# An attention-and-feed-forward kernel on one core: a first unit with an order of its own, weight splits at other places, and layer norms measured and turned at other times

## The chip, the cores and the metric

The kernel runs on one core of one Trainium2 chip. The metric is the device time of one execution in microseconds (us), as the median of several runs. The engines are named as in the profile: PE (TensorE, matmuls), DVE (VectorE), ACT (ScalarE), POOL (GpSimd) and SP (SyncE, which here only issues transfers).

## The reference

The input x has 4 batches of 512 tokens and 512 features. The kernel adds two blocks to it.

```python
x = x + attn(layernorm(x))
x = x + ffn(layernorm(x))

# attn, with H = 16 heads, DK = 64, DV = 128, M = 64 slots
q, k, v, s, g = h @ Wq, h @ Wk, h @ Wv, clip(h @ Ws, -32, 32), h @ Wg
z  = cumlogsumexp(s over tokens);  p = exp(s - z);  decay = exp(z_prev - z)
hk_t = hk * decay_t + k_t p_t      # state 64 x 64 per head
ok_t = q_t hk_t;  pv = softmax(ok) # over the 64 slots
hv_t = hv * decay_t + p_t v_t      # state 64 x 128 per head
o_t  = pv_t hv_t
o = o * rsqrt(mean(o*o) + 1e-5) * g_norm_weight * silu(g)
attn = o @ Wo

# ffn, 512 -> 1536 -> 512, weights rounded to float8_e4m3 first
ffn = (silu(h @ gate * gs) * (h @ up * us)) @ down * ds
```

All values are float32.

## The kernel before

**Units.** Attention is cut into 32 units. A unit is one group g of two heads (g from 0 to 7) for one batch b. The first half goes through all groups with batches 0 and 1 in turn: unit 0 is (g 0, b 0), unit 1 is (0, 1), unit 2 is (1, 0), and so on to unit 15, which is (7, 1). Units 16 to 31 do the same with batches 2 and 3. A unit with even g also computes the values v for two groups, so it is longer. After unit 31 comes the feed-forward block: 4 batches, each in 12 chunks of 128 hidden features.

**A unit.** The function `attention` writes a unit down in this order: projections s (`slots`), k (`keys`) and q (`queries`); transposes of e = exp(s) and k; for even g the four parts of v (`values`); the states and masked products of the first recurrence (`key_states`, `query_key`); the gate g of two heads (`gate_main`, `gate_mixed`, `gate_silu`); `slot_scores` (ok), the softmax, the second recurrence and `read_out` (ov). The output of the unit before is finished inside the next one: `scale_output`, `turn_output`, `high_output` and `split_output` make its oT, and `project_output` multiplies by Wo (ps_o in the profile; `add_output` adds ps_o_m and sends y to the `stream` in DRAM with an accumulating transfer of POOL).

**Precision.** A float32 product is made of three products in fp32r. A weight or an activation is split into a high part, a low part and a third one, called less. A projection is then eight matmuls of high and low parts (`main`, ps_g for instance) and four with the third (`mixed`, ps_g_m). A projection has its own PSUM tile from a pool of three (ps3, "proj"), so a third one after `main` waits until ACT has evicted the first. Unit 0 alone multiplies in plain float32 (`whole`), with the raw weights and with `xn_whole`, the normed tokens.

**Weight splits.** `load_matrix(nm, g, True)` splits a matrix in pieces of 512 columns: `high` on ACT (L245) and `rest`, two operations on DVE (L252 and L257), so w_s, w_k and w_q have one piece, w_g and w_o two, w_v four. The raw matrix comes by `fetch`, two buffers in turn. The split matrix is also stored to DRAM (split_*), and the second half loads it from there (L231).

**Layer norms.** `layernorm(b, which)` measures each of the four 128-token chunks (`measure`: three DVE operations and a power on POOL), normalises (xn), transposes on PE (ps_xn) and splits the result in `parts` (xs; DVE L349 and L351, ACT L354). x_0 is measured and turned before anything else. x_2 is measured in unit 14 and turned in unit 15. x_3 is loaded and measured at the start of unit 16. x_0 of the second norm is measured in unit 30.

**Order.** Nothing is scheduled by a tool: with `tc.manual_schedule` each engine carries out its instructions in the order in which they are written. Two lists fill that order. `work` holds pieces of weight splits, layer norm measures, xs parts and the rounding of feed-forward weights: `other(n)` carries out the next n pieces (or `pace[0]` of them), and `need(name)` goes on until no piece of that name is left. `steps` holds the transposes of a layer norm, one chunk in each `next_step()`. In the second half the feed-forward weights are rounded to float8 in such pieces on DVE (`quantize`) and stored to `rounded`.

Of the kernel before, what the change touches and what calls it, by code (L numbers as in the profile page):

```python
# [49 lines left out]
def kernel(  # L50
# [18 lines left out]
    nc = tc.nc  # L69
# [101 lines left out]

    def need(key):

        while any(name == key for name, _ in work):
            other(1)
# [31 lines left out]
    def fetch_first():  # L207

        for tag, names in (("og", "sk"), ("oT", "q"), ("w_o", "g")):
            w = one.tile([P, 2, RAW // 2], F32, tag=tag, name=f"raw_{names}")  # L210
# [8 lines left out]
            if names == "q":  # L219
                fetch()  # L220
                fetch()

    def load_matrix(nm, g, first):
# [23 lines left out]
        def rest(n):  # L247
# [10 lines left out]
            if (n + 1) * 512 % RAW == 0 or n + 1 == pieces:  # L258
                if g > 0 or nm in "vo":
                    fetch()  # L260
# [12 lines left out]
        work.append((nm, lambda: high(0)))  # L273
# [22 lines left out]
    def layernorm(b, which, n_bank=None):  # L296
# [33 lines left out]
        def transposes(n):  # L330
# [6 lines left out]
            if which == 1:  # L337
# [5 lines left out]
        def parts(n):  # L343
# [3 lines left out]
            if start:  # L347
                src = whole[0][:, :, cols]
            nc.vector.tensor_tensor(lo, src, hi, ALU.subtract)  # L349
# [6 lines left out]
        if start:  # L356
            for n in range(NT):
                measure(n)
                if n > 0:
                    normalise(n - 1)  # L360
                    transposes(n - 1)
            normalise(NT - 1)
# [6 lines left out]
        at = max([i + 1 for i, (name, _) in enumerate(work) if name in ("v", "g", "q")], default=0)  # L369
# [139 lines left out]
    def project(nm, b, name, to, between=None):  # L509
        if name == f"{nm}_0_0":  # L510
            p = Projection(nm, b, 0, name).whole()
            other({"s": 6, "k": 2, "q": 2}[nm])
# [85 lines left out]
    class Heads:  # L598
# [195 lines left out]
        def split_output(self, h):  # L794
# [4 lines left out]
            )  # L799
            nc.scalar.mul(lo, lo.bitcast(F32), 1.0 / DELTA)  # L800
# [30 lines left out]
    def attention(g, b, before, load):  # L831
# [5 lines left out]
        def output(n):  # L837
            if before:
                before.project_output(n)
                before.add_output(n)  # L840
# [6 lines left out]
        if before:  # L847
            need(f"xs_{b}")
            need("s")
# [4 lines left out]
        if before:  # L854
            before.scale_output()
            need("k")

        def running_sum():
            if before:
                before.scale_other()  # L860
# [7 lines left out]
        if before:  # L868
            need("q")
        X.queries(other if before and (even or steps) else None)  # L870
        load("q")
        X.turn_e()
        if even:
            X.turn_k()
            if before:
                need(f"xs_{b}")
                need("v")
                need("xs_0")
            X.values(0)
            if before:  # L880
                before.turn_output(0)
# [4 lines left out]
            next_step()  # L886
            if before:
                before.high_output(0)
                before.split_output(0)
                before.turn_output(1)  # L890
            X.query_key()
            X.values(2)
            if before:
# [305 lines left out]
```

## Time and profile before

| | before |
|---|---|
| median of 3 runs | 1541.26 us (1541.14 to 1542.71) |
| the profiled execution | 1541.84 us, of which the span of the core is 1540.0 |
| mean granted TensorE clock | 0.987 |
| idle time of PE | 68.5 us |
| DVE, ACT, POOL busy | 72%, 46%, 13% of the span |
| chain that ended last | PE 81%, DVE 13%, ACT 4%, issue 2% |
| DMA | 212.5 MB, mean 138 GB/s |

The span is the stretch from the first to the last instruction of the core; 1.84 us of the execution lie around it. The page counts the time that an engine worked. A busy PE need not be at full speed: PEclk is the clock granted to it, in tenths. A unit's place in time is read from the first ps_s of the unit in the timeline of PE.

### The profile page before, as it was taken

The page shows a single profiled execution, that of the slowest core. Times are in us where ns is not written, and L with a number is a line of the kernel's source. Part 1 is how long each engine was busy: PE and PEld are TensorE (multiplying, and loading weights), DVE is VectorE, ACT ScalarE, POOL GpSimd, SP SyncE. Part 2 cuts the span into 40 slices and gives each one's busy share as a digit, 9 for nine tenths or more (in the row PEclk, how much of TensorE's full clock was granted, in tenths as well). Part 3 has the DMA queues.
Part 4 walks back from the last instruction along what each step waited for, and adds up shares of the span by engine and source line. Part 5 has one row for each costly group of instructions (what it writes and reads, how often), then busy time and mean ns, then how long its engine had stood idle before and what let it go on. Part 6 is the DMA issues. An engine that isn't in the chain of part 4 may idle for free.

```text
span 1540.0 us, 23008 instructions
## 1 busy us (share of the span) xinstructions
PE 1471.5 (96%) x9053; PEld 1180.2 (77%) x9053; DVE 1109.0 (72%) x1968; ACT 708.3 (46%) x1214; POOL 193.0 (13%) x204
## 2 busy tenths in 40 slices
PE   7897999999999999699999999999999999999998
PEld 3576778778887887577778877887888778888886
DVE  5676767886788678757788888888888865444333
ACT  3544454655555455434554454444544543222222
POOL 2001101111121102101110111111111211000000
PEclk9998999999999999989999999999999999999999
DMA  6235645475557464505673668265836562101000
GB/s 233 103 116 164 180 157 153 118 214 189 160 130 230 123 243 106 178 1 151 192 200 68 178 187 222 63 244 137 234 99 234 125 195 28 38 18 55 1 28 28
DMA packets 80715, 212.52 MB, mean 138 GB/s; under 512 B 6152, under 2 KB 34848, under 8 KB 75424
## 3 DMA queue, kind: packets, MB, share of 16 engines
q1 hardware_dynamic: 61792, 176.96, 31.4%
q0 software_dynamic: 18528, 33.58, 15.1%
q8 instruction: 71, 1.16, 0.3%
q10 hardware_dynamic: 288, 0.52, 0.1%
q14 instruction: 36, 0.29, 0.1%
HBM read 107.23 MB, written 108.00 MB: 140 GB/s over the span
## 4 chain that ended last, share of the span: by engine, by line
PE 81%; DVE 13%; ACT 4%; issue 2%; DMA 0%; POOL 0%; DVEq 0%; POOLq 0%; ACTq 0%
PE ps_o L810 8%; PE ps_v L540 7%; PE ps_fg L970 5%; PE ps_fu L970 5%; PE ps_ov L737 4%; PE ps_o_m L810 4%; PE ps_g L480 4%; PE ps_v_m L540 3%; PE ps_q L480 3%; PE ps_g_m L503 3%; PE ps_s L480 3%; PE ps_k L480 3%; PE ps_fd L1014 2%; PE ps_a L567 2%; PE ps_fe L1014 2%; PE ps_b L567 2%
## 5 line engine op out<-in xcount | busy, mean ns | idle before, releaser
L826 POOL DMA_DIRECT2D stream<-y x128 | 110.9, 869 | 933.4 <-DVE y L825 901.3
L810 PE MATMUL ps_o<-w_o,oT 128*128 128x512 f32 x512 | 150.5, 413 | 6.0 <-DVE w_o L252 5.2
L820 ACT ACTIVATE y<-ps_o 128x512 f32<-128x512 f32 x128 | 76.7, 599 | 134.2 <-PE ps_o L810 132.4
L480 PE MATMUL ps_g<-xs,w_g 128*128 128x512 f32 x496 | 127.2, 398 | 5.9 <-ACT w_g L245 5.3
L540 PE MATMUL ps_v<-w_v,xs 128*128 128x512 f32 x480 | 126.2, 405 | 0.0
L991 DVE SCALAR_TENSOR_TENSOR h<-ps_fu,scol,act 128x512 f32<-128x512 f32 x48 | 36.0, 750 | 108.3 <-PE ps_fu L970 107.0
L480 PEld LDWEIGHTS ps_g<-xs,w_g 128*128 128x128 f32 x496 | 92.6, 190 | 27.4 <-ACT w_g L245 5.9
L810 PEld LDWEIGHTS ps_o<-w_o,oT 128*128 128x128 f32 x512 | 89.7, 189 | 26.2 <-DVE w_o L252 6.8
L540 PEld LDWEIGHTS ps_v<-w_v,xs 128*128 128x128 f32 x480 | 87.6, 190 | 19.6 <-issue 0.2
L800 ACT ACTIVATE oT<-oT 128x512 fp32r<-128x512 f32 x64 | 40.6, 634 | 130.9 <-DVE oT L797 130.9
L970 PE MATMUL ps_fg<-xs,wf 128*128 128x512 f32 x384 | 96.8, 394 | 2.0 <-DVE xs L349 2.0
L970 PE MATMUL ps_fu<-xs,wf 128*128 128x512 f32 x384 | 95.0, 389 | 0.0
L825 DVE TENSOR_TENSOR y<-y,ps_o_m 128x512 f32<-128x512 f32 x128 | 87.3, 682 | 8.4 <-ACT y L820 5.5
L970 PEld LDWEIGHTS ps_fg<-xs,wf 128*128 128x128 f32 x384 | 71.1, 188 | 16.7 <-DVE xs L349 2.3
L970 PEld LDWEIGHTS ps_fu<-xs,wf 128*128 128x128 f32 x384 | 72.1, 188 | 15.2
L810 PE MATMUL ps_o_m<-w_o,oT 128*128 128x512 f32 x256 | 81.0, 396 | 1.7 <-ACT y L820 1.7
L507 DVE TENSOR_TENSOR sg<-sg,ps_g_m 128x512 f32<-128x512 f32 x62 | 42.6, 687 | 45.2 <-PE ps_g_m L503 42.3
L549 DVE TENSOR_TENSOR v<-v,ps_v_m 128x512 f32<-128x512 f32 x60 | 41.2, 686 | 46.9 <-PE ps_v_m L540 42.6
L997 ACT CAST both<-h 128x512 fp32r<-128x512 f32 x48 | 30.0, 624 | 96.6 <-DVE h L991 96.6
L480 PE MATMUL ps_s<-xs,w_s 128*128 128x512 f32 x248 | 66.1, 408 | 8.5 <-ACT xs L354 8.5
L503 PE MATMUL ps_g_m<-xs,w_g 128*128 128x512 f32 x248 | 68.7, 399 | 4.5 <-ACT sg L485 4.5
L752 POOL TENSOR_TENSOR rs<-rs,mhalf 128x8 f32<-128x8 f32 x32 | 58.9, 1839 | 103.4 <-DVE rs L749 95.5
(165 smaller groups left out, 3216.9 us busy)
## 6 DMA issues: line engine op xcount, KB each, us to landing
stream<-y POOLq DMA_DIRECT2D x128, 256.0 KB, 5.8
split_v<-w_v SPq DMA_DIRECT2D x4, 3072.0 KB, 11.4
split_g<-w_g SPq DMA_DIRECT2D x8, 1536.0 KB, 7.1
split_o<-w_o SPq DMA_DIRECT2D x8, 1536.0 KB, 6.2
w_v<-split_v SPq DMA_DIRECT2D x4, 3072.0 KB, 15.4
w_g<-split_g SPq DMA_DIRECT2D x8, 1536.0 KB, 6.7
w_o<-split_o SPq DMA_DIRECT2D x8, 1536.0 KB, 10.1
rounded<-qw SPq DMA_DIRECT2D x36, 256.0 KB, 4.2
```

The costliest lines, as they stand in the source:

```text
L480: nc.tensor.matmul(self.p, products(self.nm, c, self.col0, i), xs[self.b][i][:, c, :], start=(i == 0 and c == 0), stop=(i == 1 and c == KC ...
L503: nc.tensor.matmul(self.m, products(self.nm, c, self.col0, 2), xs[self.b][2][:, c, :], start=(c == 0), stop=(c == KC - 1),)
L540: nc.tensor.matmul(dst, xs[b][i][:, c, n * P : (n + 1) * P], wt["v"][:, i, c * 2 * HV : (c + 1) * 2 * HV], start=(i == which[0] and c == 0 ...
L567: nc.tensor.matmul(pa[h][:, n, :], lT[rows, cols], rT[rows, cols], start=True, stop=True)
L737: nc.tensor.matmul(po[h][:, n, :], self.bb[h][:, n, :], both_v[self.b][:, n, self.v0 + h * DV : self.v0 + (h + 1) * DV], start=False, stop ...
L752: nc.gpsimd.tensor_tensor(rs, rs, mhalf.rearrange("p (h n) -> p h n", h=HG), ALU.pow)
L810: nc.tensor.matmul(dst, self.oT[:, i, h, n * P : (n + 1) * P], wt["o"][:, i, h * D : (h + 1) * D], start=(i == which[0] and h == 0), stop= ...
L820: nc.scalar.mul(y, p, 1.0 + DELTA)
L825: nc.vector.tensor_tensor(y, y, m, ALU.subtract)
L826: nc.gpsimd.dma_start(stream[self.b][n * P : (n + 1) * P, :], y, accum_op=ALU.add)
L970: nc.tensor.matmul(pp, w[:, c * P : (c + 1) * P], xs[b][k][:, c, :], start=(c == 0 and k == 0), stop=(c == KC - 1 and k == 1),)
L1014: nc.tensor.matmul(sums[n], parts[k][:, n * P : (n + 1) * P], fw[c][2], start=(c == 0 and k == 0), stop=(c == NFC - 1 and k == 1),)
```

## The change

- `first_unit` writes unit 0 down by itself. The first part of its values is computed between the second and the third transpose of x_0, the second before s; the gate of the first head comes before ok, that of the second after the softmax. The raw Wv is fetched ahead of Ws, Wk and Wq, and all four chunks of x_0 are loaded from SP. The high part of xs_0 is made from `xn_whole` in `parts`, no longer right after the transpose.
- The splits of the first weights are queued at the start of unit 0 (s, k, q, v, then the parts of xs_0, then g; o later), and carried out along units 0 and 1. `piece` carries out the high part and the first rest of a matrix together. Odd-g units begin with `piece()` in place of two `other(1)`, and `pace` is 2 only at unit 1 and at unit 16. So the later splits of the first half also stand at other places: that of g for unit 14 directly before its gate, that of o in unit 15 directly before ps_o.
- `split_output` gives its ACT scaling to `low_output`; in odd-g units it is written behind `gate_main(0)`.
- x_2 is measured from unit 13 on and turned from `gated()` of unit 14, which stands between the gate's projections and `gate_silu`. x_3 is loaded and queued at `gated()` of unit 15, and turned in unit 16. The second norm of x_0 is measured from unit 29 on and turned from `gated()` of unit 30.

```diff
                 work.pop(0)[1]()
+    def piece():
+        while work:
+            name, run = work.pop(0)
+            run()
+            if not name.endswith("_"):
+                break
     def need(key):
...
     def fetch_first():
+        fetch()
+        fetch()
         for tag, names in (("og", "sk"), ("oT", "q"), ("w_o", "g")):
+            if names == "g":
+                load_tokens(1, x)
             w = one.tile([P, 2, RAW // 2], F32, tag=tag, name=f"raw_{names}")
...
                 )
                 raw[nm, 0] = [to]
-            if names == "q":
-                fetch()
-                fetch()
...
             nc.vector.scalar_tensor_tensor(w[:, 2, cols], hi, DELTA, lo, ALU.mult, ALU.subtract)
             if (n + 1) * 512 % RAW == 0 or n + 1 == pieces:
-                if g > 0 or nm in "vo":
+                if g > 0 or nm == "o":
                     fetch()
...
             rest(n)
-        work.append((nm, lambda: high(0)))
+        work.append((nm + "_", lambda: high(0)))
         work.extend((nm, lambda n=n: step(n)) for n in range(pieces))
...
             if start:
                 src = whole[0][:, :, cols]
+                nc.scalar.mul(dst[0][:, :, cols], src, UNDER)
             nc.vector.tensor_tensor(lo, src, hi, ALU.subtract)
...
                     normalise(n - 1)
                     transposes(n - 1)
+                if n == 2:
+                    between()
             normalise(NT - 1)
...
         todo.insert(2, (key + "0", lambda: normalise(0)))
         todo.insert(4, (key + "1", lambda: normalise(1)))
-        at = max([i + 1 for i, (name, _) in enumerate(work) if name in ("v", "g", "q")], default=0)
+        at = max([i + 1 for i, (name, _) in enumerate(work) if name in ("v", "g", "q") or name[:3] == "xs_"], default=0)
         work[at:at] = todo
...
         if name == f"{nm}_0_0":
             p = Projection(nm, b, 0, name).whole()
-            other({"s": 6, "k": 2, "q": 2}[nm])
             nc.scalar.mul(to, p, QSCALE if nm == "q" else 1.0)
...
                 less, lo.bitcast(F32), -1.0 / DELTA, hi.bitcast(F32), ALU.mult, ALU.add
             )
+        def low_output(self, h):
+            lo = self.oT[:, 1, h, :]
             nc.scalar.mul(lo, lo.bitcast(F32), 1.0 / DELTA)
...
         nc.scalar.preload_act_table_set("natural_log_exp_and_others")
-    def attention(g, b, before, load):
+    def first_unit():
+        X = Heads(0, 0)
+        parts = layernorm(0, 1, between=lambda: X.values(0))
+        for nm in "skqv":
+            load_matrix(nm, 0, True)
+        transposing = layernorm(1, 1)
+        work.extend(parts)
+        load_matrix("g", 0, True)
+        for _ in range(5):
+            piece()
+        X.values(1)
+        X.slots()
+        other(2)
+        X.keys(X.running_sum)
+        other(4)
+        X.queries(None)
+        X.turn_e()
+        X.turn_k()
+        piece()
+        piece()
+        X.values(2)
+        X.key_states()
+        piece()
+        X.inverse()
+        X.values(3)
+        fetch()
+        fetch()
+        load_matrix("o", 0, True)
+        transposing()
+        next_step()
+        other(2)
+        X.query_key()
+        next_step()
+        other(2)
+        X.gate_main(0)
+        piece()
+        X.slot_scores()
+        X.value_states()
+        next_step()
+        X.softmax()
+        X.softmax_exp()
+        other(1)
+        next_step()
+        other(1)
+        X.gate_main(1)
+        X.slot_weights()
+        X.gate_silu(0)
+        X.gate_silu(1)
+        exp_and_log()
+        X.weight_slot()
+        X.softmax_sum()
+        need("xs_0")
+        X.read_out()
+        return X
+    def attention(g, b, before, load, gated):
         X = Heads(g, b)
         even = g % 2 == 0
         def output(n):
-            if before:
-                before.project_output(n)
-                before.add_output(n)
+            before.project_output(n)
+            before.add_output(n)
         def early_step():
             if not any(name.endswith("_m") for name, _ in work):
                 next_step()
-        if before:
-            need(f"xs_{b}")
-            need("s")
+        need(f"xs_{b}")
+        need("s")
         X.slots()
         load("s")
         if not even:
             early_step()
-        if before:
-            before.scale_output()
-            need("k")
+        before.scale_output()
+        need("k")
         def running_sum():
-            if before:
-                before.scale_other()
+            before.scale_other()
             X.running_sum()
...
             before.split_output(1)
             X.inverse()
-        if before:
-            need("g")
-            X.gate_main(0)
-            X.gate_mixed(0)
-            if even:
-                other()
-                next_step()
-            X.gate_main(1)
-            X.gate_mixed(1)
-            load("g")
-            if even:
-                load("v")
-            X.gate_silu(0)
-            X.gate_silu(1)
-            exp_and_log()
+        need("g")
+        X.gate_main(0)
+        if not even:
+            before.low_output(0)
+            before.low_output(1)
+        X.gate_mixed(0)
+        if even:
+            other()
+            next_step()
+        X.gate_main(1)
+        X.gate_mixed(1)
+        load("g")
+        if even:
+            load("v")
+        gated()
+        X.gate_silu(0)
+        X.gate_silu(1)
+        exp_and_log()
         X.slot_scores()
         X.value_states()
-        if not before:
-            next_step()
-            X.gate_main(0)
         X.softmax()
         other()
-        if before:
-            need("o")
-            before.project_output(0)
+        need("o")
+        before.project_output(0)
         X.softmax_exp()
-        if before:
-            before.add_output(0)
-            before.project_output(1)
-        else:
-            X.gate_main(1)
-            X.gate_silu(0)
-            X.gate_silu(1)
-            exp_and_log()
-            load("v")
-            load("g")
+        before.add_output(0)
+        before.project_output(1)
         X.slot_weights()
-        if before:
-            before.add_output(1)
+        before.add_output(1)
         X.softmax_sum()
-        if before:
-            next_step()
+        next_step()
         output(2)
...
         x1[0] = one.tile([P, NT, D], F32, tag="y", name="x1_0")
         for n in range(NT):
-            (nc.scalar if n % 2 else nc.sync).dma_start(x1[0][:, n, :], blocks[:, n, :])
+            nc.sync.dma_start(x1[0][:, n, :], blocks[:, n, :])
         exp_and_log()
         fetch_first()
-        parts_0 = layernorm(0, 1)
-        for nm in "skq":
-            load_matrix(nm, 0, True)
-        load_tokens(1, x)
         for b in range(2):
             nc.sync.dma_start(stream[b], x[b])
         load_scales()
         units = [(g, b) for b0 in range(0, B, 2) for g in range(NG) for b in (b0, b0 + 1)]
-        before = None
+        before = first_unit()
+        scale_columns()
         to_come = [3 * NFC]
-        for i, (g, b) in enumerate(units):
-            last = i + 1 == len(units)
+        for i, (g, b) in enumerate(units[1:], 1):
             def load(nm):
                 after = (i + 1 + 2 * (nm == "v")) // 2 * 2
-                if i == 0:
-                    if nm in "vgo":
-                        load_matrix(nm, 0, True)
-                    if nm == "v":
-                        work.extend(parts_0)
-                    return
                 if b == B - 1 and after == len(units):
                     for c, tag in enumerate(PLACES):
                         if tag == f"w_{nm}":
                             load_ffn(c)
                 elif nm == "o":
-                    if b % 2 == 0 and i > 0:
+                    if b % 2 == 0:
                         load_matrix("o", g, i < len(units) // 2)
                 elif b % 2 == 1 and after < len(units):
                     n = units[after][0]
                     load_matrix(nm, n // 2 if nm == "v" else n, after < len(units) // 2)
+            def gated():
+                pace[0] = 1 + (pace[0] > 1 and i > 1)
+                if g == NG - 1 and b % 2 == 0:
+                    transposing[0]()
+                elif (g, b) == (NG - 1, 1):
+                    need("xs_2")
+                    load_tokens(3, x)
+                    transposing[0] = layernorm(3, 1)
...
             if (g, b) == (NG - 2, 2):
                 load_tokens(0, stream)
+            if (g, b) in ((NG - 2, 1), (NG - 2, 3)):
+                transposing = [layernorm(*((2, 1) if b == 1 else (0, 2)))]
             if (g, b) == (0, 2):
-                load_tokens(3, x)
-            if i == 0 or (g, b) == (0, 2):
-                layernorm(b + 1, 1)()
-            elif (g, b) in ((NG - 1, 0), (NG - 1, 2)):
-                transposing = layernorm(*((2, 1) if b == 0 else (0, 2)))
-            elif g == NG - 1:
-                transposing()
-            if (g, b) == (0, 2):
+                transposing[0]()
                 assert not to_fetch
                 stage()
             if b > 1:
                 for _ in range(min(0 if units[i] == (0, 2) else 2 if g % 2 else 4 if b == 2 else 3, to_come[0])):
                     work += [("round", f) for f in quantize()]
                     to_come[0] -= 1
-            pace[0] = 2 if steps else 1
-            if before:
+            pace[0] = 2 if i == 1 or (g, b) == (0, 2) else 1
+            if g % 2:
+                piece()
+            else:
                 other(1)
                 other(1)
-            before = attention(g, b, before, load)
-            while steps:
-                next_step()
-            if i == 0:
-                scale_columns()
+            before = attention(g, b, before, load, gated)
         dsc = one.tile([P, D], F32, tag="qT", name="dsc")
```

## The prediction, on record before the result

> **What bounds the kernel now.** I read the page first: the busy row of TensorE (PE), then the forty slices.
>
> ```profile
> span 1540.0 us, 23008 instructions
> PE 1471.5 (96%) x9053; PEld 1180.2 (77%) x9053; DVE 1109.0 (72%) x1968; ACT 708.3 (46%) x1214; POOL 193.0 (13%) x204
> ...
> PE   7897999999999999699999999999999999999998
> ...
> PEclk9998999999999999989999999999999999999999
> ```
>
> PE is the bound: 96%, 68.5 us idle. The low digits lie at the start (slices 1 to 5) and in slice 17 (about 650 us), where the granted clock dips too. So the work that DVE and ACT do elsewhere is hidden, and only these two places can pay. Next the waits of PE, its own list, columns "waited for: total, times, longest":
>
> ```profile
> PE ps_s L480 <- ACT xs L354: 8.5, 1, 8.5
> PE ps_xn L333 <- DVE xn L326: 7.8, 3, 7.1
> PE ps_g L480 <- ACT w_g L245: 5.3, 2, 5.1
> PE ps_o L810 <- DVE w_o L252: 5.2, 5, 1.5
> PE ps_q L480 <- ACT w_q L245: 5.0, 2, 2.5
> PE ps_g_m L503 <- ACT sg L485: 4.5, 15, 0.4
> PE ps_k_m L503 <- ACT eT L485: 3.9, 1, 3.9
> PE ps_a L567 <- DVE xs L349: 3.2, 1, 3.2
> ```
>
> Seven of the eight are single stalls; one (ps_g_m) comes back in every odd-g unit. The timeline places them. On PE, the bracket is the idle time before the row:
>
> ```profile
> 68.44 2.07 PE L503 MATMUL ps_k_m<-xs,w_k 128*128 128x512 f32 x4 [3.91 <-ACT eT L485]
> 135.07 3.78 PE L480 MATMUL ps_g<-xs,w_g 128*128 128x512 f32 x8 [5.09 <-ACT w_g L245]
> ...
> 654.60 2.08 PE L480 MATMUL ps_s<-xs,w_s 128*128 128x512 f32 x4 [8.46 <-ACT xs L354]
> ...
> 677.83 3.78 PE L540 MATMUL ps_v<-w_v,xs 128*128 128x512 f32 x8
> ```
>
> A warm group of eight takes 1.98 to 2.1 us; the eight at 135.07 and 677.83 take 3.78. A long stall is paid twice: once idle, once at half clock. Last, the SyncE queue (SP) ahead of the 8.46 us stall:
>
> ```profile
> 628.29 0.32 SPq L231 DMA_DIRECT2D w_g<-split_g  x1
> 634.45 0.32 SPq L265 DMA_DIRECT2D split_o<-w_o  x1
> 634.82 0.43 SPq L291 DMA_DIRECT2D x<-_attn_hidden_states_dram  x1
> ```
>
> The 1 MB load of x_3 starts at 634.82 and lands 9.6 us later.
>
> To price stalls with their half clock, I take the distance between the first ps_s of consecutive units. Undisturbed, an even-g unit (with values) takes 41.8 us, an odd-g unit 31.7 (first batch of the pair) or 32.7 (second). Measured: unit 0 ends at 59.7; unit 1 53.7 (excess 11.9), unit 2 42.7 (11.0), unit 3 37.6 (4.9), unit 4 44.6 (2.8), unit 15 37.4 (4.7), unit 16 62.9 (21.1, of which 1.4 is x_3's four transposes). Together 56 us.
>
> **What the Trainium skill says.** "TensorE: Matmul & The Clock Gate", section "Part 1: The HAM clock gate": after an idle window of about 3.4 us the array goes to half clock, and needs about 3.4 us of sustained work to get the full one. The trace agrees: after the stalls the clock is down for 3.41 us (from 122.5), 6.83 (67.9, 132.7 and 675.4) and 10.24 (648.0). The same page, "Engine queue depths", has ACT and DVE strictly first in, first out; so does the trace, where ACT's eviction of eT (68.44 above) stands behind four w_v splits that start at 58.36. "Trainium Kernel Development and Optimization", section "Key Constraints": transfers issued from SP, ACT and POOL share 16 DMA engines, and a second issuer saves issue time only. So x_0's chunks all on SP cost two issues, 0.4 us each, hidden behind the first two chunks' measures.
>
> **The change part by part.** PE and DVE issue the same instructions in both kernels. ACT gives two DMA issues to SP. All is order.
>
> *Start.* In the old order the first projection, s, begins at 12.89, after all four transposes of x_0 (from 7.10 on) and 0.67 for ACT's copy. Now v_0_0 needs only two of them: they end at 9.67, so v_0_0 begins near 10.3. raw_v, now issued ahead of s, k and q at about 2.1 and 2.9 instead of 3.34 and 4.2, lands 6.8 later, at 8.9 to 9.7, in time. But the other eight transposes (2.17) are moved behind v_0_0 and not saved; what goes is the idle between groups, 0.4, and, as PE works densely from 10.3 on, perhaps one cold window of 3.41 us (the clock rose at 16.7), worth 1.7. I take −2 (+1 if raw_v lands with s's traffic at 11.5; −4 if the windows fall well).
>
> *Units 1 to 4.* W_V's eight DVE operations (0.65 each) and four ACT highs (0.62 each) leave the end of unit 0 for its early part, where PE runs 3.5 us whole-fp32 projections and DVE has room. W_G is split at the end of unit 0, W_O in unit 1, each ahead of its use. In exchange x_0's parts now end unit 0 (four DVE operations, 2.7 us), and w_g's two highs stand before eT on ACT. Unit 1: of the 11.9 excess, stay about 1.5 to 2.4 of the 3.9 stall with some half clock, and the rest of the crowded DVE (6 operations of about 0.65 between z and qT, as before). I take −6.5 (−3 to −9). Unit 2: the waits for w_q (2.5) and w_g (5.1), with 1.7 and 3.4 lost to half clock, have their cause removed, both splits done in unit 1. −10.5 of 11.0 (−6 to −11). Unit 3: w_o split before kT instead of between ok and y; −4.5 of 4.9. Unit 4: w_q's high ahead of eT, the 2.5 us wait goes: −2.5. If that cover fails, the wait for w_q's last low part, one 0.65 operation, is what is late next.
>
> *low_output.* In odd-g units the two ACT scalings of oT (0.63 each) go behind sg's eviction, which PE waits for 15 times at 0.3. Two of those units are counted above: 13 x 0.3 = −4.0. What is late next is oT itself, needed only at ps_o, 6 us later.
>
> *Units 8 and 12.* w_q's pair now stands before kT: +0.3 each, +0.5 in all.
>
> *Unit 14 (new wait).* W_G's four DVE operations leave unit 13's end, for the place between rzT and sg of unit 14. There DVE ends rzT at 593.33 in the old frame, while ps_g began at 588.08. The low parts come at 593.9 and 595.2, the last at 595.9. So the gate's main group ends near 596.0 instead of 590.0: 6.0, less 0.3 of the old sg wait, plus about 1.5 of half clock after 4 to 5 us idle: +7 (+3 to +9). Behind it wait sg, ok, and everything after.
>
> *Unit 15 (new wait).* x_3's load is moved before gate_silu. It is queued on SP behind w_g's load, which waits for PE's last ps_g_m (628.29). It is issued at about 628.7 instead of 634.8; w_g (1.5 MB, 6.3 us alone) shares the engines, so I take 9 us and a landing near 637.7 (6.3 and 9.6 bound it: 635.0 to 638.3). DVE ends ok at 633.06; the next in its queue are four measures of x_3 (1.0 each), two xn (0.5 each) and W_O's four operations (2.6). The measures wait for the load, so they end at 642.8, and W_O at 645.4. ps_o's second half waits for it: its mixed pair ends at 645.9, was 634.8. +11.1. The rest of the unit (10.2) is shorter by the 0.5 wait and two transposes (0.7), longer by about 3 of half clock after 12 us idle. +12.9; I take +13 (+7 to +16).
>
> *Unit 16.* Its xs_2 is ready. The stall of 8.46, that of 3.16 at 675.85, and both cold stretches go. ACT's y wait (1.7) and the transposes remain: 62.9 to about 45.4, −17.5 (−13 to −19).
>
> *Feed-forward start.* The old waits of 0.5 and 2.0 for xs_0 go, but eight quantising operations (about 5 us) come in front of h_0 on DVE. 0 (−2 to +2).
>
> **Sum**: −2.0 −6.5 −10.5 −4.5 −2.5 −4.0 +0.5 = −29.5 for the first half; +7 +13 −17.5 = +2.5 for the handover. −27.0. The profiled execution took 1541.84 (span 1540.0); it becomes 1514.8. That execution is 0.6 above the median, so **1514.2**.
>
> **Rivals.** *The handover pays.* x_3 lands at 635, PE's clock stays up, and unit 14's gate waits only 3: units 14 and 15 cost +3 and +7 instead of 20, and the rest holds. That is 10 less: 1504.2. For it: x chunks of 256 KB landed in 4.1 us. Against it: the measures and W_O alone are 7.6 us of DVE in front of ps_o.
>
> *The splits only change place.* The operation counts are the same; DVE in unit 1 is 77% busy (41.1 of 53.7 us). If the stalls of units 1 to 3 come back at kT and qT in half their size, 21.5 becomes 10.7: 1525.0. Against it: unit 2 was 70% busy, and it is not the load but one position in ACT's queue that made its waits.
>
> *Slower: x_3 comes very late.* One mechanism: DVE is in order, and the measures stand ahead of W_O and y in unit 15, so PE loses one us for each us that x_3 lands later than my 637.7. The gain of 27 is gone at a load of 36 us; 45 us give 1550.2. Against it: the longest median landing on the page is 15.4 (w_v, 3 MB), and x_3 took 9.6 in the same traffic.
>
> *That the change does not do what it says* is the second rival at its full size for the first half: nothing but the start and the sg waits, −2.0 −4.0 +0.5 +2.5 = −3.0, 1538.3.
>
> **How the numbers follow.** Forecast 0.62 (1505 to 1523), handover pays 0.16, splits change place 0.17 (with 0.03 for the full size), slower 0.04, about nothing 0.01. 0.2% is 3.1 us, about what a measurement of this kernel can tell from no change. Faster 0.94, same 0.02, slower 0.04. The range reaches into both neighbours: 1499 to 1529.
>
> **What would show it.** Right: first ps_v near 10.3 and unit 1's first ps_s near 57.7; unit 2 of about 32 us; no ps_g_m wait for sg; a new PE wait of 4 to 6 us for w_g in unit 14, and one of 7 to 13 us for w_o in unit 15, with DVE's first measure of x_3 waiting about 4.6 us for a DMA; unit 16 of about 45 us without ps_s or ps_a waits. Wrong: w_q or w_g waits left in unit 2, kT or qT late in unit 1, a short ps_o wait in unit 15 (then 1504), or one beyond 20 us.

## The result, and the profile after

The changed kernel takes 1537.36 us (median of 12, 1535.66 to 1540.92), the kernel before 1541.49 beside it (12 runs): ratio 0.9973, interval 0.9964 to 0.9982. It is 4.1 us faster, where 27 were forecast. The profiled execution took 1536.70, its span is 1534.7 (5.3 less than before).

The page of the changed kernel, busy row of PE, its forty slices and the clock:

```profile
span 1534.7 us, 23020 instructions
PE 1462.3 (95%) x9053; PEld 1177.2 (77%) x9053; DVE 1109.1 (72%) x1968; ACT 710.4 (46%) x1214; POOL 192.7 (13%) x204
...
PE   8899999999999978799999999999998899999998
...
PEclk9999999999999999899999999999999999999999
```

The digits at the start rose from 7897 to 8899. The dip at slice 17 is still there and wider (7, 8, 7 from slice 15 on), and a dip is new at slices 31 and 32. The sum of PE's idle time rose from 68.5 to 72.4 us (1534.7 − 1462.3), so the kernel is not faster because PE waits less: PE is busy for 9.2 us less with the same 9053 matmuls. The mean granted clock of 0.989, which was 0.987, makes about 3 of that (an estimate, 0.002 of 1540); e6 below shows another part, rows that overlap again. The waits of PE, columns "waited for: total, times, longest":

```profile
PE ps_o L825 <- DVE w_o L262: 10.1, 2, 9.6
...
PE ps_g L493 <- DVE w_g L262: 4.8, 2, 4.6
...
PE ps_q L493 <- DVE w_q L264: 3.1, 3, 1.6
...
```

The old list's stalls at ps_s (8.5) and ps_a (3.2) are gone, and so are the fifteen waits of ps_g_m for sg. Waits for w_q, w_g and w_o are still there in name, but at another place in time. The distance between the first ps_s of consecutive units, from the timeline of PE, says where (us; for unit 31 up to the first ps_fg, then to the end of the span):

| stretch | before | after | difference | forecast |
|---|---|---|---|---|
| start of unit 1 | 59.70 | 58.43 | −1.3 | −2 |
| unit 1 | 53.67 | 47.85 | −5.8 | −6.5 |
| unit 2 | 42.66 | 31.08 | −11.6 | −10.5 |
| unit 3 | 37.63 | 31.04 | −6.6 | −4.5 |
| unit 4 | 44.64 | 42.99 | −1.7 | −2.5 |
| units 8 and 12 | 83.59 | 88.03 | +4.4 | +0.5 |
| units 5, 6, 7, 9, 10, 11, 13 | 254.1 | 249.6 | −4.4 | in −4.0 |
| unit 14 | 31.67 | 42.33 | +10.7 | +7 |
| unit 15 | 37.35 | 53.96 | +16.6 | +13 |
| unit 16 | 62.93 | 47.82 | −15.1 | −17.5 |
| units 17 to 29 | 483.0 | 481.9 | −1.2 | in −4.0 |
| unit 30 | 31.69 | 38.33 | +6.6 | 0 |
| unit 31 | 34.17 | 37.16 | +3.0 | 0 |
| first ps_fg to the end | 283.2 | 284.2 | +1.0 | 0 |

Each column is one execution. Stretches without a new wait agree within 0.1 us from run to run. The others do not: unit 0, written the same in ten further profiles below, takes 57.2 to 59.6, and unit 8 43.7 to 46.9 in the runs that leave its order alone.

Up to unit 14 the changed kernel is 26.9 us ahead (575.94 against 549.04). The handover, units 14 to 16, costs 12.2 of it, and the tail from unit 30 on another 10.6. On PE's timeline of the changed kernel, the bracket again the idle time before the row:

```profile
557.29 2.12 PE L493 MATMUL ps_q<-xs,w_q 128*128 128x512 f32 x8 [2.51 <-ACT w_q L255]
569.92 1.07 PE L493 MATMUL ps_g<-xs,w_g 128*128 128x512 f32 x2 [4.56 <-DVE w_g L262]
...
601.27 1.08 PE L343 MATMUL ps_xn<-ident,xn 128*128 128x128 f32 x4 [3.68 <-DVE xn L336]
...
632.41 0.80 PE L825 MATMUL ps_o<-w_o,oT 128*128 128x512 f32 x1 [9.61 <-DVE w_o L262]
...
1184.74 3.57 PE L493 MATMUL ps_q<-xs,w_q 128*128 128x512 f32 x8 [4.00 <-DVE eT L520]
```

Two of these, the waits for w_g and w_o, are the ones that the forecast announced. The other three it did not have. DVE's timeline shows what makes the longest:

```profile
621.64 0.69 DVE L704 TENSOR_TENSOR ok<-ps_okn,mx 128x512 f32<-128x512 f32 x1
626.68 0.69 DVE L329 BATCH_NORM_STATS2 stats<-x 128x6 f32<-128x512 f32 x1 [4.35 <-DMA x<-_attn_hidden_states_dram]
...
631.66 0.69 DVE L262 TENSOR_TENSOR w_o<-raw_o,w_o 128x512 fp32r<-128x512 f32 x1
```

After ok DVE waits 4.35 us for x_3's load (issued at 617.94, landed in 8.7), measures for 5.0, and only then splits w_o, for which PE has waited since 622.8. The tail has the same pattern. First the SP queue, then DVE:

```profile
1161.85 0.32 SPq L241 DMA_DIRECT2D w_g<-split_g  x1
1162.21 2.04 SPq L473 DMA_DIRECT2D wf<-rounded  x4
1164.35 0.41 SPq L421 DMA_DIRECT2D qw<-in_L_ffn_gate_w_dram  x1
```

```profile
1183.32 0.43 DVE L437 TENSOR_SCALAR q<-qw 128x512 int32<-128x512 int32 x1 [6.52 <-DMA qw<-in_L_ffn_gate_w_dram]
...
1184.00 0.68 DVE L520 TENSOR_TENSOR eT<-eT,ps_s_m 128x512 f32<-128x512 f32 x1
```

A raw feed-forward weight of 256 KB is issued behind 4.5 MB on the same queue and lands after 18.9 us. The rounding piece that needs it stands in front of eT on DVE, and with eT the whole of unit 30. In the kernel before the same four loads were issued at 1178.1, and of the rounding only one last store came after them:

```profile
1178.09 2.26 SPq L460 DMA_DIRECT2D wf<-rounded  x4
1189.44 0.32 SPq L438 DMA_DIRECT2D rounded<-qw  x1
```

### The profile page after: what moved, and what is told of

It reads as the page before. It is cut to its first block, busy times and chain, and to the rows that moved or that the text cites. A ratio compares the mean times of both kernels' runs of the same rounds, so it can differ in the third digit from the quotient of the medians.

```text
span 1534.7 us, 23020 instructions
## 1 busy us (share of the span) xinstructions
PE 1462.3 (95%) x9053; PEld 1177.2 (77%) x9053; DVE 1109.1 (72%) x1968; ACT 710.4 (46%) x1214; POOL 192.7 (13%) x204
## 4 chain that ended last, share of the span: by engine, by line
PE 81%; DVE 9%; DMA 5%; ACT 3%; issue 1%; SPq 0%; DVEq 0%; ACTq 0%
PE ps_o L825 7%; PE ps_v L552 7%; PE ps_g L493 7%; PE ps_fg L1023 5%; PE ps_fu L1023 5%; PE ps_q L493 4%; PE ps_g_m L516 3%; PE ps_o_m L825 3%; PE ps_ov L749 3%; PE ps_v_m L552 3%; PE ps_s L493 3%; PE ps_k L493 2%; PE ps_fd L1067 2%; PE ps_fe L1067 2%; PE ps_a L579 2%; PE ps_b L579 2%
## 5 line engine op out<-in xcount | busy, mean ns | idle before, releaser
L825 PE MATMUL ps_o<-w_o,oT 128*128 128x512 f32 x512 | 149.7, 413 | 11.1 <-DVE w_o L262 10.1
L493 PEld LDWEIGHTS ps_g<-xs,w_g 128*128 128x128 f32 x496 | 92.1, 189 | 26.9 <-DVE w_g L262 6.0
L1023 PEld LDWEIGHTS ps_fu<-xs,wf 128*128 128x128 f32 x384 | 72.1, 188 | 15.2
L498 ACT ACTIVATE sg<-ps_g 128x512 f32<-128x512 f32 x62 | 37.1, 599 | 98.6 <-PE ps_g L493 98.6
L493 PE MATMUL ps_q<-xs,w_q 128*128 128x512 f32 x248 | 66.7, 412 | 9.9 <-DVE eT L520 4.3
L1041 ACT ACTIVATE act<-ps_fg,scol 128x512 f32<-128x512 f32 x48 | 33.0, 688 | 80.3 <-PE ps_fg L1023 80.3
## 6 DMA issues: line engine op xcount, KB each, us to landing
w_v<-split_v SPq DMA_DIRECT2D x4, 3072.0 KB, 15.2
```

What stands on the lines that cost most here:

```text
L493: nc.tensor.matmul(self.p, products(self.nm, c, self.col0, i), xs[self.b][i][:, c, :], start=(i == 0 and c == 0), stop=(i == 1 and c == KC ...
L825: nc.tensor.matmul(dst, self.oT[:, i, h, n * P : (n + 1) * P], wt["o"][:, i, h * D : (h + 1) * D], start=(i == which[0] and h == 0), stop= ...
L1023: nc.tensor.matmul(pp, w[:, c * P : (c + 1) * P], xs[b][k][:, c, :], start=(c == 0 and k == 0), stop=(c == KC - 1 and k == 1),)
```

## The experiments

My theory after the result: each lost stretch has its own cause, a piece of other work that stands in DVE's or ACT's queue directly before something PE needs. The rival to it: DVE and ACT are simply full there, so a piece taken away from one place makes the same wait at the next. All ratios are to the kernel before, run beside. Differences to the changed kernel, and between experiments, are differences of medians that were taken at different times; the kernel before lay between 1541.5 and 1542.2 then, so I read them to about 1 us.

### The handover, one cause at a time

**e1: x_3's load alone earlier.**

```diff
+        keyed()
         need("q")
         X.queries(other if even or steps else None)
...
                     need("xs_2")
-                    load_tokens(3, x)
```

In unit 15 `keyed()` issues the load, after the projection k.

> The changed kernel, with x_3's load alone moved: it is issued in unit 15 right after x_2's last chunk has been normalised (ahead of w_q's and w_g's loads) and not at gated(). In the changed kernel it is issued at 617.9 and lands 8.7 us later, and DVE's first measure waits 4.35 us for it. Theory (DVE is in order, and its queue ahead of w_o is the load's wait plus 7.6 us of work): the wait of 4.35 goes, PE's wait for w_o falls from 9.6 to about 5.2, unit 15 is 4.4 shorter (54.0 to 49.6), and the whole kernel 4 to 5 us faster. Rival (the load is the cause, what stands behind it would have fitted): w_o's wait falls below 1 us and unit 15 by 9 us or more. Rival (the transfers only change places): the load collides with w_q's, and nothing is won.

1534.55 us, ratio 0.9953 (0.9939 to 0.9968). On PE's timeline the wait for w_o is what the first theory gave:

```profile
631.80 0.80 PE L825 MATMUL ps_o<-w_o,oT 128*128 128x512 f32 x1 [5.16 <-DVE w_o L262]
```

Unit 15 falls from 53.96 to 49.12, by 4.8. The whole gained 2.8; in this execution units 8 and 14 were 3.1 and 2.4 longer than in the changed kernel's, at waits that this edit does not touch (in unit 14 the waits for w_q and w_g are the same 2.5 and 4.6, but the rows behind them ran slower), so I rest the verdict on the row and on unit 15.

**e2: w_o split ahead of the measures.**

```diff
-... if name in ("v", "g", "q") or name[:3] == "xs_"] ...
+... if name in ("v", "g", "q", "o") or name[:3] == "xs_"] ...
```

> The changed kernel, with the measures of a layer norm queued behind W_O's splits too (one name more in the list of names that layernorm puts itself behind). In unit 15 DVE then splits w_o right after ok and measures x_3 after b. Theory: PE's wait for w_o falls from 9.6 to about 1.5 to 2.5 (its four operations of 0.65), the clock stays up, unit 15 falls by 9 to 11 us; unit 16 grows by 1 to 2, as two measures now stand before its kT. Whole kernel 7 to 10 us faster. Rival (the wait only moves on): x_3's measures come so late that unit 16 waits for xs_3 or kT as long as unit 15 did for w_o, and the whole changes by less than 3 us.

1525.76 us, ratio 0.9901 (0.9884 to 0.9917): 11.6 faster than the changed kernel. On PE:

```profile
621.14 0.50 PE L825 MATMUL ps_o<-w_o,oT 128*128 128x512 f32 x1 [0.18 <-DVE w_o L262]
622.47 0.50 PE L825 MATMUL ps_o<-w_o,oT 128*128 128x512 f32 x1 [0.83 <-DVE w_o L262]
```

9.6 became 1.0, and a record takes 0.50 again instead of 0.80. Unit 15 falls by 9.8 (44.15), unit 16 stays (47.87). The measures cost nothing where they now stand, behind b: x_3 has landed by then. So the order on DVE was the cause, and the load only lengthened it. Of the 11.6, 9.8 lie in unit 15; 1.3 of the rest is an earlier start of unit 1, which this edit does not touch.

**e3: unit 13 with pace 2.**

```diff
-            pace[0] = 2 if i == 1 or (g, b) == (0, 2) else 1
+            pace[0] = 2 if i in (1, 13) or (g, b) == (0, 2) else 1
```

> The changed kernel, with pace 2 in unit 13, so that w_s, w_k, w_q and w_g of group 7 are split within unit 13 and none in unit 14. Theory (x_2's measures took the slots of unit 13, and the splits fell into unit 14 just before their use): PE's waits in unit 14 for w_q (2.5) and w_g (4.8) go, with the half clock after them; unit 14 goes from 42.3 to 31.1 to 32, unit 13 grows by 0 to 1.5. Whole kernel 9 to 11 us faster. Rival (DVE of unit 13 cannot take them): unit 13 grows by 5 us or more, since its v or oT come late behind the splits.

1528.63 us, ratio 0.9913 (0.9898 to 0.9927): 8.7 faster than the changed kernel. Unit 14 falls from 42.33 to 32.57, unit 13 grows from 41.78 to 44.46, more than the theory's 0 to 1.5 and less than the rival's 5. Both waits of unit 14 were splits that x_2's measures had pushed out of unit 13; unit 13 has room for most of them.

### The tail, and the missing piece

**e4: the second norm of x_0 back at its old place.** The edit puts `layernorm(0, 2)` at unit 30 and its turns at the start of unit 31.

> The changed kernel, with the second norm of x_0 measured in unit 30 and turned in unit 31, as in the kernel before; all else as changed. In the changed kernel unit 30 takes 38.3 (31.7 before), unit 31 37.2 to the first ps_fg (34.2 before). Theory (measures from unit 29 on push the rounding of the feed-forward weights back, so that a rounding piece stands in DVE's queue in front of eT and waits 6.5 us for its raw weights, whose load was issued behind four weight loads and took 18.9): the stall in unit 30 goes, 6 to 7 us. Rival (odd-g units carry out one piece fewer at their start, since piece() stops after one rounding piece where two were carried out): the rounding stays late, and at least half of the 10 us of the tail stays.

1534.45 us, ratio 0.9956 (0.9943 to 0.9968): 2.9 faster. Unit 30 is back at 31.10, but unit 29 is now 46.27 (41.84), because a rounding piece waits there. On DVE:

```profile
1148.95 0.43 DVE L437 TENSOR_SCALAR q<-qw 128x512 int32<-128x512 int32 x1 [2.83 <-DMA qw<-in_L_ffn_down_w_dram]
```

From the start of unit 29 to the end of the span it is 397.5 us, against 390.9 before and 401.5 in the changed kernel. Only 4.0 of 10.6 came back: this run's rival, the missing piece, had it.

**e5: two pieces at the start of every unit again.**

```diff
-            if g % 2:
-                piece()
-            else:
-                other(1)
-                other(1)
+            other(1)
+            other(1)
```

> The changed kernel, with piece() at the start of odd-g units replaced by the two other(1) of the kernel before; norms and all else as changed. piece() ends after one piece unless that piece is a high part, so an odd-g unit begins with one piece fewer: W_Q slips from units 7 and 11 into 8 and 12 (2.0 and 2.4 us longer), w_q's high in unit 14 stands behind rzT on ACT (2.5 us), and in the second half the rounding ends a unit later. Theory (the missing piece is the cause of these): units 8 and 12 fall by 2 each, unit 14 by 2 to 4 (w_g's wait of 4.6 stays), units 30 and 31 by 3 to 9 together: 9 to 14 us faster than the changed kernel. Rival (the earlier measures are the cause): unit 30 keeps its stall of 6 to 7, unit 14 its 42: not more than 5 us faster.

1522.39 us, ratio 0.9869 (0.9853 to 0.9885): 15.0 faster than the changed kernel, the largest gain of a single edit to it. From unit 29 to the end it is 390.4: in sum the whole tail is back, with x_0's measures still in their new place (unit 30 keeps 33.98, and the stretch from ps_fg on is 280.8). Units 8 and 12 are back at 41.87 and 41.80, and unit 15 falls by 3.2, as the xn that PE waited for at 601.27 is now normalised at the end of unit 14. The piece fewer had a good side too: units 3, 7 and 11 take 32.0 here and 31.0 with one piece (units 7 and 11 take 32.0 in all of e8 to e12 too, which begin with two). Unit 14 went the other way, to 47.5, and here the expectation was wrong by sign. On PE, then on ACT:

```profile
553.47 1.20 PE L516 MATMUL ps_k_m<-xs,w_k 128*128 128x512 f32 x4 [3.61 <-ACT eT L498]
```

```profile
552.30 0.63 ACT L255 ACTIVATE w_q<-raw_q 128x512 fp32r<-128x512 f32 x1 [6.37 <-DMA raw_q<-in_L_attn_Wq_dram]
552.83 0.58 ACT L498 ACTIVATE eT<-ps_s 128x512 f32<-128x512 f32 x1
```

w_q's high now stands ahead of eT on ACT, so a wait of 3.6 replaced one of 2.5, and half clock follows it. This is not the rival's full queue: ACT stood idle for 6.4 us first, because the raw Wq was issued at 542.95 and took 9.3 to land. It is the first theory's case again, work that waits for a transfer, put ahead of what PE needs. Of the edits tried, pace 2 in unit 13 (e3) and the old place of x_2's measures (e8) take the waits out of unit 14.

### The first half

**e6: low_output undone**, its scaling back in `split_output`.

> The changed kernel with low_output's scaling put back into split_output, all else as changed. Theory (each odd-g unit pays two waits of 0.3 of ps_g_m for sg): units 3, 6, 7, 10, 11, 18, 19, 22, 23, 26, 27 are each 0.6 longer (31.7 instead of 31.1), about 8 to 9 us over 15 units. Rival (one wait of 0.3 in each, as the forecast had it): 0.3 each, 4 to 5 us.

1547.00 us, ratio 1.0031 (1.0020 to 1.0042): 9.6 slower than the changed kernel by the medians (8.9 by the two ratios), and slower than the kernel before. Eleven odd-g units without another new wait take 31.6 to 31.7 instead of 31.0 to 31.1, which makes 9.0 over 15 such units. The list of waits shows one wait of 0.3 in each, so the first theory's number was right and its reason, two waits, was not. The rows of the kernel before (unit 14) and of the changed one (unit 15) show how 0.3 costs 0.6:

```profile
590.93 1.98 PE L480 MATMUL ps_g<-xs,w_g 128*128 128x512 f32 x8
593.21 1.20 PE L503 MATMUL ps_g_m<-xs,w_g 128*128 128x512 f32 x4 [0.30 <-ACT sg L485]
594.33 0.87 PE L668 MATMUL ps_ok<-qT,sk 64*64 64x128 f32 x12
```

```profile
614.65 1.98 PE L493 MATMUL ps_g<-xs,w_g 128*128 128x512 f32 x8
616.47 1.07 PE L516 MATMUL ps_g_m<-xs,w_g 128*128 128x512 f32 x4
617.47 0.87 PE L680 MATMUL ps_ok<-qT,sk 64*64 64x128 f32 x12
```

From ps_g to ps_ok it is 3.40 with the wait and 2.82 without. In these rows the end of ps_g overlaps the start of ps_g_m where nothing is waited for, and after the wait it does not.

**e7: s first in unit 0**: `values(0)` and `values(1)` behind `turn_k`, the transfers as changed.

> The changed kernel, in which unit 0 computes s, k and q first and v_0_0 and v_0_1 after the transposes of k; the transfers, splits and all else stay as changed. In the changed kernel the first ps_v starts early, but the raw Wv is in front of Ws, Wk and Wq on SP, and unit 1 begins at 58.43 (59.70 before). Theory (only the idle time between the transposes and a cold window can be won): unit 1 begins 1 to 2.5 us later than in the changed kernel, as s must wait for all four transposes and for its own weights behind 1 MB of Wv. Rival (the values-first order wins nothing, the gain is in what ends unit 0): unit 1 begins within 0.3 us of 58.43.

1539.73 us, ratio 0.9983 (0.9976 to 0.9990). Unit 1 begins at 60.20 instead of 58.43, 1.8 later. PE's first row of s is at 12.21 and takes 5.72, where v of the changed kernel started at 9.49. But in the ten other profiles with the changed kernel's unit 0, unit 1 begins anywhere from 57.16 to 59.60, so one execution does not settle 1.8. The medians say 2.4, the ratios 1.5, with intervals that touch. That the values-first order wins something is likely; its size is open, and so is how much of the 1.3 in the table is its own.

**e12: Wv's splits late**, queued behind the parts of xs_0 (on top of e9 below).

> e9_pace1 with Wv's splits queued behind the parts of xs_0 again, as in the kernel before; first unit, order of PE and all else as in e9. Two of the four pieces of w_v are then split at the end of unit 0, one high part of Wv and Wg's stand before eT on ACT in unit 1, and w_o moves behind v. Theory (the early places of Wv's splits are what shortened unit 1): unit 1 grows from 47.8 by 3 to 6 with a longer wait of ps_k_m for eT and half clock after it, unit 2 stays at 31; whole kernel 3 to 6 us slower than e9. Rival (unit 1 was shortened by the removal of xs_0's parts from it, not by Wv): unit 1 within 1 us of 47.8.

1500.92 us, ratio 0.9741 (0.9715 to 0.9766), 5.0 slower than e9 (its four runs lie between 1497.4 and 1505.2, so the size is rough). The sum fits the theory, the place does not. In e9 unit 1 has this on PE:

```profile
66.61 1.20 PE L516 MATMUL ps_k_m<-xs,w_k 128*128 128x512 f32 x4 [3.26 <-ACT eT L498]
```

and in e12, in units 0 and 1:

```profile
43.91 1.12 PE L343 MATMUL ps_xn<-ident,xn 128*128 128x128 f32 x4 [3.18 <-DVE xs L360]
...
75.09 0.65 PE L569 MATMUL ps_kn<-ident,kT 128*128 128x128 f32 x4 [2.90 <-DVE kT L520]
```

Unit 1 is even 0.6 shorter (47.20), but begins 4.5 later. Its stall of 3.3 at eT has become one of 2.9 at kT, and unit 0 has a stall of 3.2 that e9 does not have. So unit 1 keeps a stall of about 3 in either order, as the rivals say (full queues, and Wv not the cause in unit 1); the early places of Wv's splits spare unit 0 one, and are worth 3.9 over both units (106.4 against 110.2).

### A better version

**e8: first half of the change, norms, pace and unit starts of before.** Out of `gated` go the turns and x_3's load; they return to the starts of units 15, 16 and 31.

> The changed kernel with the layer norms of x_2, x_3 and x_0 (second) measured and turned where they were before, the old pace and the old two pieces at the start of odd-g units; first unit, early splits, low_output and the rule that puts a norm's measures behind xs parts stay. Theory (the new first half is worth 27 us, and the handover and tail gave most of it back): units 0 to 13 as in the changed kernel less 4 for units 8 and 12, units 14 and 15 as before or 1 shorter (31 and 36 to 37), tail as before. Unit 16: xs_2's parts now stand ahead of x_3's measures on DVE, so the stall of 8.5 at its first ps_s goes and 2 to 4 come back at eT and kT, 48 to 53 instead of 62.9. Span 1497 to 1504. Rival (unit 16 stalls as before): span 1508 to 1513. Rival (the first half's gain depends on the new places of the norms): more than 1518.

1510.34 us, ratio 0.9790 (0.9775 to 0.9805); span 1507.6, where 1497 to 1504 was expected. Units 14, 15 and 16 take 31.1, 36.8 and 50.8, as the theory said. What was missing lies elsewhere: units 2, 3 and 4 take 38.6, 36.9 and 44.6, since the old rule gives unit 1 a pace of 1.

**e9: pace 2 in unit 1 put back.**

```diff
-            pace[0] = 2 if steps else 1
+            pace[0] = 2 if i == 1 or steps else 1
```

> e8_old_norms with pace 2 in unit 1 put back (e8 had the old rule for the pace, which gives 1 there). In e8 units 2, 3 and 4 took 38.6, 36.9 and 44.6, with waits of 4.3 for w_g and 3.0 for w_o. Theory (it is the double pace of unit 1 that keeps w_g and w_o of the first groups out of units 2 and 3): units 2, 3 and 4 go to 31.1, 32.0 and 41.8, the rest as in e8 (unit 14 31.1, unit 15 36.8, unit 16 50.8): 15 to 17 us faster than e8, span 1490 to 1493. Rival (the early splits in unit 0 alone do it, and unit 1 pays for the double pace): unit 1 grows by 3 us or more and the whole wins less than 10.

1495.94 us, ratio 0.9698 (0.9681 to 0.9714): 14.4 faster than e8. Units 2, 3 and 4 take 31.14, 32.01 and 41.80, unit 1 stays at 47.84. These three units gain 15.2: the double pace of unit 1 is thus worth a little over half of the 26.9 that the first half won. The profiled span, 1497.2, is above the expected 1490 to 1493, 2.9 of it in unit 16.

**e11: x_3's load at gated() of unit 15**, on top of e9.

> e9_pace1 with x_3's load issued at gated() of unit 15 instead of at the start of unit 16. Theory: in e9 the stall at unit 16's first ps_s (2.7) is x_2's last part behind DVE's queue, not the load, so nothing changes by more than 1 us. Rival (the first measure of x_3 waits for its load there too): unit 16 is 2 to 4 us shorter.

1495.38 us, ratio 0.9694 (0.9679 to 0.9708): the same as e9 within the intervals, and the stall of 2.7 at unit 16's ps_s stays. Unit 16 takes 52.1, and in e8, e9 and e12, whose order there is one and the same, 50.8, 53.7 and 50.8. The stall is the same in all four, the row behind it is not. In e8, then in e9:

```profile
633.35 1.20 PE L493 MATMUL ps_s<-xs,w_s 128*128 128x512 f32 x4 [2.67 <-ACT xs L365]
```

```profile
618.29 2.08 PE L493 MATMUL ps_s<-xs,w_s 128*128 128x512 f32 x4 [2.67 <-ACT xs L365]
```

The mean granted clock of the 10 us around and after this row is 1.00 in e8 and e12, 0.85 in e11 and 0.68 in e9. So the spread is half clock, which follows the same stall in some executions and not in others.

**e10: x_2's norm sooner on top of e11**, with pace 2 in unit 13.

> e11_load_early with x_2 measured from unit 13 and turned from gated() of unit 14, as in the changed kernel, and pace 2 in unit 13; x_3 is measured at the start of unit 16. Theory (the sooner norm of x_2 is good if the splits of unit 13 and w_o are not pushed in front of their use): unit 13 44 to 45, unit 14 31 to 33, unit 15 36 to 44 with a wait of about 1.5 for w_o, unit 16 46 to 49 without a stall at ps_s; the four together 158 to 168 against 160.5 in e8. Rival (a real gain): under 157. Rival (the x_2 turns themselves cost in unit 15, as the changed kernel's 3.7 wait of ps_xn shows): 165 or more.

1501.76 us, ratio 0.9737 (0.9723 to 0.9752). Units 13 to 16 take 44.55, 32.55, 42.15 and 48.43, together 167.7 against 161.9 in e11: within the theory's range, but also within the second rival's (165 or more), and 6 slower. The rival's cause is there: in unit 15 PE waits 3.2 for kn behind x_2's parts, a wait that e11 does not have. x_2's sooner norm shortens unit 16, and units 13 to 15 pay more than that for it.

So e9 and e11 are faster than the kernel before by 3.0 to 3.1%, and than the changed one by 2.7%. No run puts e2, e3 and e5 together on the changed kernel. The page of e11:

```profile
PE 1453.3 (97%) x9053; PEld 1173.2 (79%) x9053; DVE 1106.3 (74%) x1968; ACT 709.8 (48%) x1214; POOL 192.2 (13%) x204
```

Its span is 1493.7 us and its idle time 40.4, where it was 68.5 and 72.4.

## Why the prediction was right and wrong

It was wrong: 1514.2 forecast with a range of 1499 to 1529, measured 1537.4. The sign was right. By the profiled spans, 21.7 of the 27.0 are missing: 10.6 in the tail, 9.7 in the handover, 3.9 in units 8 and 12, less 2.5 by which the other terms came out better.

**Right: the first half.** The forecast up to the end of unit 4 was −26.0, measured −26.9, and no step of it is off by more than 2.1. The reason for it was only partly right: 7.5 of unit 2's gain hang on unit 1's pace (e8, e9), of which the prediction says nothing, and the early places of Wv's splits spare the new unit 0 a stall, while unit 1 keeps one (e12). The eT stall of the kernel before was read too simply: ACT had finished the four w_v splits by 60.6 and then stood idle for 5.8 us on a part of xs that waited for DVE, with eT behind it. Also loose is "seven of the eight are single stalls": by the same lines ps_o has five waits and ps_q two.

**Right in kind, too small: the new waits of units 14 and 15.** DVE's wait for x_3 was put at 4.6 and measured 4.35; w_g's at 4 to 6, measured 4.8; w_o's at 7 to 13, measured 10.1 at two rows. What the sums lack are waits beside these. In unit 14, w_q's high behind rzT on ACT (2.5). In unit 15, the last xn of x_2 behind z, xs and kT on DVE (3.7), and then a late kn (1.5 and 0.7). Both come from x_2's work being spread over units that already split weights. The step that makes the rest of unit 15 shorter by a wait and "two transposes" looked at PE's instructions and not at what those transposes wait for. Unit 16 gained 15.1 instead of 17.5; a wait of 1.5 of ps_oT for a part of xs is new there, the rest is open. Together the handover came to +12.2 instead of +2.5.

**Failed: "Units 8 and 12, +0.5".** They cost 4.4, and e5 gave it back. The step saw that w_q moved, priced the wait at 0.3, and did not ask why it moved: `piece()` ends after one piece where two were carried out before.

**Failed: "Feed-forward start, 0".** The tail cost 10.6, a term that the sum put at nothing. The step counted eight late rounding operations and their effect on h_0, and did not walk back to the units in which they are late. e4 and e5 place the cause: the missing piece delays the rounding by a unit, and its raw weights then load behind 4.5 MB.

**Too small, in favour: low_output, −4.0.** e6 gives 8.9 to 9.6. The term took the listed wait of 0.3 as its price, and start to start it is 0.6. Against the kernel before, units with a new wait of their own hide a part (units 21 and 22 lose 1.8, which e5 takes back), and 1.0 each of what units 7 and 11 gained comes from the one piece fewer, not from low_output.

Of the rivals, "the splits only change place" named the right mechanism but the wrong units: work that only changes its place is what units 8, 12 and 14 and the tail show (in the tail it is the rounding), not units 1 to 3. Its full size, 1538.3, lies within 1 us of the result, but by luck: it had the first half gain nothing, and the first half gained 26.9 and lost it later. The slower one, a very late x_3, was there at its small size only.

The prediction took half clock to follow idle windows of about 3.4 us. Here a stall of 2.67 was enough in two executions of four (e9 and e11), so a price for a stall is a range, not one number.

## What to carry to other kernels

When an order is written by hand, a change of one filler rule (here one piece fewer at the start of half of the units) moves work in every unit, also in stages that the change does not mention. So compare where each moved piece stands on each engine up to the very end, and for each ask what is queued behind it there and how old its data is. And be wary of filler that may wait for a transfer ahead of the work PE needs next: DVE's measures in unit 15, the rounding in unit 30 and e5's split of w_q are three cases here, and one name in a list was worth 9.8 us in unit 15.

## What I had not expected of the hardware

A wait listed with 0.3 us cost 0.58 from start to start, as the rows of a group that nothing holds up overlap those of the next in the trace. One and the same stall of 2.67 us was followed by full clock in two executions and by half clock in two others, which made its unit longer by 0, 0, 1.4 and 2.9 us. The transfers of the raw feed-forward weights, 256 KB each, had a median of 2.8 us to landing from 1100 us on; one took 18.9 when it was issued behind 4.5 MB on the same queue, and in e4 one that followed the same loads took 16.3.
